# One chunk of a weight matrix, loaded behind a small write of VectorE

## The chip, the cores and the metric

The kernel runs on one core of one Trainium2 chip. The metric is the device time of one execution in microseconds, and its median over several runs. A core has five engines that each work through a queue of their own: TensorE (PE in the profile, with its weight loads as PEld), VectorE (DVE), ScalarE (ACT), GpSimd (POOL) and SyncE (SP). An engine waits for another by semaphores. Transfers between the device memory and the core's own memory are issued from the queues of SP, ACT and POOL, and carried by 16 DMA engines that all queues share.

## The reference

Inputs: x (8 x 1024 x 512), a condition (8 x 512), and weights. The first layer makes a matrix of its own for every one of the 8 batches, a base plus a term of rank 8; the second scales the columns and rows of a weight W by values made from the condition. Both are residual:

```
h = gelu(layernorm(cond) @ w1 + b1)
x_a, x_b = split(h @ w2 + b2)                    # 512 x 8 each, per batch
layer = base + x_a @ x_b.T                       # per batch
x = x + (x + x @ layer)
ys = cond / sqrt(512)
d = rsqrt((ys * ys) @ (W * W) + 1e-8)
x = x + ((x * ys) @ W) * d
```

Everything is float32. With I the identity, the whole of it is x @ P for each batch, with P = (2 I + base + x_a x_b^T) (I + diag(ys) W diag(d)).

## The kernel before

The kernel forms P for each batch and multiplies x by it. Float32 products are made of three: each operand is split into a rounded part (names with h, such as nh, bh, ph) and the rest (nl, bl, pl), and h x h, h x l and l x h are added up in the accumulators of PE. The rounded part is a copy or a scaled copy by ACT, the rest a subtraction by DVE. A matrix of 512 rows lies as 4 chunks of 128 rows, `[:, k, :]` for k = 0 to 3.

Up to line 886 the order of the instructions of ACT, DVE and SP is the order in the source: `ve`, `se` and `sy` are wrappers that pin each instruction behind the one before on the same engine (lines 52 to 64), and PE's matmuls are pinned by `mm` (line 44). Behind line 886, in the main part, the order on ACT, DVE and POOL is left to a planner. The framework sets all semaphores by itself, from what each instruction reads and writes; a transfer into a tile that an earlier instruction writes waits for that instruction, on the queue that issues the transfer.

The start, in the order of the source:

- Loads. From ACT's queue: chunk 0 of W into `w_sb` (line 89, 256 KB), and, behind ACT's first activation, chunk 1 (line 124, 256 KB). From SP's queue: `sm` (small things: the condition in columns, an identity), chunks 0 and 1 of the transposed base (`b_raw`), the condition, chunks 2 and 3 of W, chunks 2 and 3 of the base, and w1 (lines 90 to 97). Behind them on the same queue go the 16 loads of w2, 1 MB each, issued as buffers come free.
- Eleven matmuls on zeros (`keep_warm`, line 116), while the first loads are on their way.
- `ve.tensor_scalar_mul(ysT, condT, SCALE)` (line 180): ys, in columns.
- Chunk 0: POOL adds 2 I to the base's block (`twice_i`), ACT scales W's chunk by ys into `nh` (`round_yw`), ACT rounds the base into `bh` (`round_b`, for chunk 0 in three pieces), DVE makes `nl` (`rest_yw`) and `bl` (`rest_b`). Chunk 1 the same way (lines 188 to 192).
- Then ACT squares the four chunks of W into `wsq` (lines 193 and 194), and DVE makes ys squared and the layer norm of the condition; ACT's `sd` in it stands behind the squares.
- PE: twelve matmuls of chunk 0 into four accumulators `pg`, six of chunk 1 (two of the accumulators), then `pq_v` (`RowsProduct`, eight narrow matmuls that read `wsq`, for d), then the rest of chunk 1 with small transposes between, `pq_z` (for h), and chunks 2 and 3.

After that h is multiplied by w2 (the accumulators `px`, 128 narrow matmuls until about 61 us), P is formed for the first batches, and from about 72 us on the products of x with P (`po`) run, with the forming of the later P's between them. The stores of the output go out mostly from ACT's queue.

The change touches lines 124 (a load on ACT's queue, the second one of `w_sb`) and the place behind line 180.

Of the kernel before, what the change touches and what calls it, by code (L numbers as in the profile page):

```python
# [30 lines left out]
def cond_resid_kernel(ctx: ExitStack, tc: tile.TileContext, small, cond, condrows, consts,  # L31
# [32 lines left out]
    ve, se, sy = InOrder(nc.vector), InOrder(nc.scalar), InOrder(nc.sync)  # L64
# [18 lines left out]
    w_sb = cp.tile([P, KC, D], F32, name="w_sb")  # L83
# [37 lines left out]

    root = cp.tile([NB, 1], F32, name="root")
    se.activation(root, eps_l, AF.Sqrt)
    se.dma_start(w_sb[:, 1, :], weight[:, 1, :])


    hT = sp.tile([P, KC, 2, 32], F32, name="hT")
# [19 lines left out]
    def round_yw(k):  # L147

        se.mul(n0[k][0], w_sb[:, k, :], ysT[:, k, 0:1])
# [6 lines left out]
    def twice_i(k):  # L156
        blk = b_raw[:, k, k * P:(k + 1) * P]
        pin(nc.gpsimd.tensor_tensor(blk, blk, two_i, ALU.add))
# [19 lines left out]


    ve.tensor_scalar_mul(ysT, condT, SCALE)  # L180
    twice_i(0)
    round_yw(0)
    round_b(0, P, 2 * P)
# [1014 lines left out]
```

## Time and profile before

| | |
|---|---|
| time, median of 3 runs | 294.06 us (293.88 to 294.23) |
| time of the profiled execution | 293.74 us |
| its span, first to last instruction | 291.9 us |
| PE busy | 286.3 us (98%) |
| DVE, ACT, POOL busy | 214.8, 175.0, 35.9 us |
| mean granted clock of PE | 0.998 |
| DMA engines' share, 8 to 55 us | 1.00 to 1.04, at 404 to 438 GB/s |
| chunk 0 of W on ACT's queue: issued, time to landing | 0.73, 3.7 us |
| chunk 1 of W on ACT's queue: issued, time to landing | 1.24, 4.7 us |
| first main matmul (`po`) starts | 71.85 us |

A row of the timeline has the start in us, the length in us, the engine, the line, the operation, what it writes and reads, how many of its kind it stands for, and in brackets how long the engine was idle before it and what ended that. ACTq and SPq mark instructions that issue transfers. Almost everything in this kernel is issued through helpers, so the line is that of a helper (L62, L45), and tiles tell the groups apart; buffer numbers are left out. w_sb stands for W, and, where it comes from in_w, for w1. The profiled execution's own time is the span and 1.8 us around it.

### The profile page before, as it was taken

What the parts mean: (1) busy time and instruction counts of PE and PEld (TensorE: products, weight loads), DVE (VectorE), ACT (ScalarE), POOL (GpSimd) and SP (SyncE); (2) the same over time, 40 slices, a digit from 0 to 9 for tenths busy, and PEclk for the clock granted to TensorE, in tenths of its full rate; (3) what the DMA queues carried; (4) which work ended last, traced back from release to release, by engine and by line L of the source; (5) the groups of instructions that cost most, each with busy time, mean ns of one, the idle gap of its engine ahead of it and who ended that gap; (6) DMA issues with size and microseconds to landing.
All of it is one profiled execution on the core that took longest, in us unless ns stands there. A gap on an engine that the chain in (4) does not pass through costs nothing.

```text
span 291.9 us, 4100 instructions
## 1 busy us (share of the span) xinstructions
PE 286.3 (98%) x1519; PEld 225.2 (77%) x1519; DVE 214.8 (74%) x295; ACT 175.0 (60%) x272; POOL 35.9 (12%) x77
## 2 busy tenths in 40 slices
PE   7999999999999999999999999999999999999995
PEld 3665566467877878888877888887888889999994
DVE  2889898989916999519799565326789977798912
ACT  5757263286849884658654575544658745856641
POOL 2111000202944560000022000000000000000000
PEclk9999999999999999999999999999999999999999
DMA  7999999992799783332328114262175870852334
GB/s 209 405 429 413 411 403 405 390 383 90 187 321 322 235 250 116 110 145 93 159 80 263 55 72 135 83 216 74 72 251 176 291 257 1 290 204 87 142 146 144
DMA packets 19924, 62.14 MB, mean 213 GB/s; under 512 B 2736, under 2 KB 4016, under 8 KB 15552
## 3 DMA queue, kind: packets, MB, share of 16 engines
q1 hardware_dynamic: 9504, 43.76, 40.7%
q10 hardware_dynamic: 6912, 12.32, 11.5%
q0 software_dynamic: 3488, 5.79, 7.5%
q8 instruction: 12, 0.20, 0.3%
q14 instruction: 8, 0.07, 0.1%
HBM read 44.02 MB, written 17.84 MB: 212 GB/s over the span
## 4 chain that ended last, share of the span: by engine, by line
PE 96%; DMA 2%; ACT 0%; DVE 0%; SPq 0%; ACTq 0%; issue 0%
PE po L45 42%; PE pp L45 20%; PE sw L45 9%; PE px L45 5%; PE sz L45 5%; PE pg L45 4%; PE pq L45 4%; PE sv L45 2%; DMA b_raw<-in_baseT 2%; PE pr L45 1%; PE pt_t L45 1%; PE ps_t L45 0%; PE pq_v L45 0%; PE pq_z L45 0%; ACT o L62 0%; DVE o L62 0%
## 5 line engine op out<-in xcount | busy, mean ns | idle before, releaser
L45 PE MATMUL po<-ph,xs 128*128 128x512 f32 x352 | 113.7, 392 | 0.0
L45 PEld LDWEIGHTS po<-ph,xs 128*128 128x128 f32 x352 | 66.0, 188 | 15.6 <-issue 1.7
L45 PE MATMUL po<-pl,xs 128*128 128x512 f32 x176 | 68.6, 390 | 0.0
L62 ACT COPY o<-po 128x512 f32<-128x512 f32 x44 | 25.9, 588 | 35.0 <-PE po L45 35.0
L45 PEld LDWEIGHTS po<-pl,xs 128*128 128x128 f32 x176 | 33.0, 188 | 6.7
L62 DVE TENSOR_TENSOR xs<-x,xs 128x1024 fp32r<-128x1024 f32 (+1 forms) x23 | 27.0, 1176 | 15.0 <-ACT xs L62 15.0
L62 DVE TENSOR_TENSOR nl_p<-n,nh_p 128x1024 fp32r<-128x1024 f32 x21 | 25.7, 1222 | 12.4 <-ACT nh_p L62 12.4
L62 ACT CAST nh_p<-n 128x1024 fp32r<-128x1024 f32 x21 | 22.1, 1054 | 14.6 <-DVE n L62 10.9
L62 ACT CAST xs<-x 128x1024 fp32r<-128x1024 f32 x22 | 23.0, 1056 | 3.6 <-DMA x<-in_x 3.6
L62 ACT COPY q<-pp 128x512 f32<-128x512 f32 x30 | 17.4, 586 | 8.7 <-PE pp L45 8.6
L542 POOL DMA_DIRECT2D fa<-kept_a x28 | 13.8, 508 | 58.3 <-PE pr L45 54.0
L45 PE MATMUL pp<-nh_p,sh 128*128 128x512 f32 x48 | 19.0, 396 | 0.0
L45 PE MATMUL pp<-nh_p,sl 128*128 128x512 f32 x48 | 18.7, 390 | 0.0
L45 PE MATMUL pp<-nl_p,sh 128*128 128x512 f32 x48 | 18.7, 390 | 0.0
L62 DVE SCALAR_TENSOR_TENSOR n<-w_sb,ysT,d 128x512 f32<-128x512 f32 x24 | 16.9, 748 | 0.9 <-DMA d<-d_out 0.9
L62 ACT CAST sh<-sraw 128x1024 fp32r<-128x1024 f32 (+1 forms) x14 | 12.9, 926 | 6.8 <-DVE sraw L62 6.8
L62 DVE TENSOR_TENSOR sl<-sraw,sh 128x1024 fp32r<-128x1024 f32 (+1 forms) x14 | 14.9, 1067 | 2.2 <-ACT sh L62 2.2
L62 DVE TENSOR_TENSOR pl<-q,ph 128x1024 fp32r<-128x1024 f32 (+1 forms) x10 | 11.1, 1116 | 6.9 <-ACT ph L62 6.9
L45 PE MATMUL px<-w,hT 128*32 128x512 f32 x128 | 15.6, 599 | 0.0
L62 ACT COPY o<-sw 128x512 f32<-128x512 f32 (+1 forms) x12 | 6.2, 518 | 15.4 <-PE sw L45 12.3
L62 DVE TENSOR_TENSOR q<-pr,q 128x512 f32<-128x512 f32 x14 | 8.8, 688 | 7.9 <-PE pr L45 7.8
L62 DVE TENSOR_TENSOR n<-n,n 128x1024 f32<-128x1024 f32 x12 | 14.5, 1225 | 0.1
(199 smaller groups left out, 576.6 us busy)
## 6 DMA issues: line engine op xcount, KB each, us to landing
w<-in_w SPq DMA_DIRECT2D x16, 1024.0 KB, 10.4
x<-in_x SPq DMA_DIRECT2D x16, 1024.0 KB, 5.6
out<-o ACTq DMA_DIRECT2D x44, 256.0 KB, 2.3
out<-o SPq DMA_DIRECT2D x8, 512.0 KB, 2.9
fa<-kept_a POOLq DMA_DIRECT2D x28, 64.0 KB, 2.7
ft<-kept_t POOLq DMA_DIRECT2D x28, 64.0 KB, 3.5
d<-d_out POOLq DMA_DIRECT2D x6, 256.0 KB, 7.3
w_sb<-in_w SPq DMA_DIRECT2D x1, 1024.0 KB, 8.5
```

The source lines that it names most:

```text
L45: tc.keep_in_program_order(nc.tensor.matmul(*args, **kw))
L62: return lambda *a, **kw: pin(f(*a, **kw)) if InOrder.on else f(*a, **kw)
L542: nc.gpsimd.dma_start(fold[name, b][32 * c:32 * c + 32, :], kept[name, g][32 * i:32 * i + 32, :])
```

## The change

The load of W's chunk 1 leaves its place behind ACT's first activation. It now stands behind ys, with a memset by DVE of one element of the chunk (row 0, column 0) ahead of it. The load writes over that zero, so it has to wait for the memset, which on DVE stands behind the instruction that makes ys. On ACT's queue the load is now ahead of the first `round_yw`.

```diff
     root = cp.tile([NB, 1], F32, name="root")
     se.activation(root, eps_l, AF.Sqrt)
-    se.dma_start(w_sb[:, 1, :], weight[:, 1, :])
...
     ve.tensor_scalar_mul(ysT, condT, SCALE)
+
+    ve.memset(w_sb[:1, 1, :1], 0.0)
+    se.dma_start(w_sb[:, 1, :], weight[:, 1, :])
     twice_i(0)
     round_yw(0)
     round_b(0, P, 2 * P)
```

What is computed is the same, and so is the number of bytes that are moved.

## The prediction

> **What bounds the kernel now.** I read the chain that ended last first, then what TensorE (PE) waits for in the whole run, then the first 13 us of ScalarE (ACT), VectorE (DVE) and PE in order of time.
>
> ```profile
> PE 96%; DMA 2%; ACT 0%; DVE 0%; SPq 0%; ACTq 0%; issue 0%
> ```
>
> The chain, by engine: from the first real matmul on it is PE. Its start, by pieces (start, length):
>
> ```profile
> 1.16 4.56 DMA b_raw<-in_baseT
> 5.73 0.02 issue
> 5.75 0.31 ACT bh L62
> 6.06 0.04 issue
> 6.10 4.54 PE pg L45 x18
> 10.64 1.00 PE pq_v L45 x8
> 11.64 0.90 PE pg L45 x3
> ```
>
> PE's own waits, all of them (total, times, longest):
>
> ```profile
> PE pg L45 <- ACT bh L62: 1.1, 1, 1.1
> PE warm L45 <- DVE eps_l L62: 1.0, 1, 1.0
> ```
>
> After 6.10 us PE is never without work: whatever holds it back early moves everything behind it, up to the end at 291.9. So the question is how late PE becomes between 6 and 11 us, and ACT decides that:
>
> ```profile
> 1.24 0.39 ACTq L62 DMA_DIRECT2D w_sb<-in_weight  x1
> 2.48 0.20 ACT L62 ACTIVATE root<-eps_l 8x1 f32<-8x1 f32 x1
> 4.49 0.72 ACT L62 ACTIVATE nh<-w_sb,ysT 128x512 fp32r<-128x512 f32 x1 [1.81 <-DMA w_sb<-in_weight]
> 5.75 0.90 ACT L62 CAST bh<-b_raw 128x128 fp32r<-128x128 f32 x3 [0.54 <-DMA b_raw<-in_baseT]
> 6.56 0.72 ACT L62 ACTIVATE nh<-w_sb,ysT 128x512 fp32r<-128x512 f32 x1
> 7.73 0.62 ACT L62 CAST bh<-b_raw 128x512 fp32r<-128x512 f32 x1 [0.45 <-POOL b_raw L158]
> 8.26 2.19 ACT L62 ACTIVATE wsq<-w_sb 128x512 f32<-128x512 f32 x4
> ```
>
> The first row is the load that is moved. Its 256 KB landed 4.7 us after issue (the landing view for issues at 1.24), at 5.94, so the second nh at 6.56, which reads it, did not wait. The squares end at 10.45, pq_v starts at 10.57: it waits 0.4 us for them. Here the chain has no slack.
>
> **The change, part by part.** *Removed:* the issue at 1.24 (0.39 us of ACT's queue). ACT then loads a table until 2.46 and idles before 4.49, so that saves nothing.
>
> *Added on DVE:* one memset of one element. The rows of the small ones are 0.06 us; it runs behind ysT:
>
> ```profile
> 0.88 0.06 DVE L62 MEMSET eps_l<- 8x1 f32 x1
> 4.04 0.18 DVE L62 TENSOR_SCALAR ysT<-sm 128x32 f32<-128x32 f32 x1 [3.10 <-DMA sm<-in_small]
> ```
>
> So it is over at 4.22 + 0.06 = 4.28. DVE's next instruction (nl, at 5.24) waits for ACT's nh: 0.9 us of idle time cover it; without that cover it would cost 0.06.
>
> *Moved:* the load now waits on ACT's queue for the memset, and every instruction of ACT behind it waits too. That wait from 2.68 to 4.28 is mostly free, since the next one, nh, waits for chunk 0 until 4.43 anyway. Taking 0.04 us from engine to engine (ACT's bh ends 6.06, PE starts 6.10), the issue runs 4.32 to about 4.72, and nh starts at 4.75, not 4.49: 0.26 late. It ends at 5.47, while bh waits for b_raw until 5.75: hidden, with 0.28 to spare. If b_raw lands earlier, because the moved 256 KB no longer share its time on the DMA engines, PE can start at most 0.28 sooner; that gain is lost again at the next wait. SyncE's queue issues the same transfers: its first w1 load, at 4.42, waits for chunk 0 alone. Some later SyncE issue may reuse the completion counter of the moved load and wait for it, but by 8.5 us w1 and four w2 loads of 1 MB each have been issued there, and b_raw's second half ahead of them lands only at 10.5: the engines stay fed.
>
> *The landing.* What is late next is chunk 1. If it lands at T, the rows give: second nh at T + 0.06 (chunk 0: landed 4.43, nh 4.49); bh 0.62 later (12.79 to 13.41, the same pair without a wait); squares 0.53 after that (7.73 to 8.26), 2.19 long; pq_v 0.12 after their end. Sum: pq_v at T + 3.52, before 10.57, so PE is late by **T - 7.05**. The other way into PE, bh and then nl and bl on DVE (0.75 + 0.69), lets the last of the six pg matmuls ahead of pq_v start at T + 3.0: under 3.52, so the squares decide. What follows pq_v (sd, drow, pa, pt_v, pq_z) shifts with it: DVE's chain hangs on sd behind the squares, and PE has no hole to make good.
>
> *How long the load takes from 4.32.* The trace has no load on an ACT queue at this moment, so bounds:
>
> ```profile
> w_sb<-in_weight ACTq DMA_DIRECT2D x2, 256.0 KB, 4.2
> out<-o ACTq DMA_DIRECT2D x44, 256.0 KB, 2.3
> d<-d_out POOLq DMA_DIRECT2D x6, 256.0 KB, 7.3
> ```
>
> From below 2.3: 256 KB on ACT's queue while the engines are mostly free (T = 6.6). From above 7.0: the first d load, issued at 26.76 on a queue of its own beside SyncE's stream of w2, with all engines busy (T = 11.3, 4.3 late). And the engines are full when the moved load comes:
>
> ```profile
> 4.50:6.00 1.50, 0.53 (x3) 0.04 (x1) 0.75 (x1) 0.96 (x3) 0.14 (x1) 1.00 1.02 367
> 6.00:8.00 2.00, 1.90 (x8) 1.51 (x9) 1.31 (x2) 1.55 (x5) 0.93 (x2) 1.00 1.01 254
> ```
>
> (the last two columns: share of the 16 DMA engines, GB/s). So the near rows are the two loads of this very tile: 3.7 for chunk 0, on an empty queue beside SyncE's, and 4.7 for chunk 1, partly behind chunk 0. I take their median, 4.2, as an estimate between them: an empty queue speaks for 3.7, the larger backlog on SyncE's queue for 4.7. T = 4.32 + 4.2 = 8.5, PE late by 8.5 - 7.05 = **1.45 us** (3.7 gives 0.97, 4.7 gives 1.97).
>
> A rule speaks against this. The Trainium skill, "DMA: Bandwidth & Descriptors", section "Anatomy of one DMA", puts a transfer at about 2.0 us plus its bytes at 436 GB/s; for 256 KB that is an estimate of 2.6 us, T = 6.9 and no loss at all (-0.1 us). The rows of this stage, 3.7 and 4.7, do not agree, with the engines 100% busy; the rule is a fit for one transfer by itself, and on another queue.
>
> **The sum.** The profiled execution took 293.74 us (span 291.9 and 1.8 around it), 0.32 under the median of 294.06. 293.74 - 0 + 0 + 1.45 = 295.19; against the median, which the new runs will be compared with, 294.06 + 1.45 = **295.5**.
>
> **The rivals.**
> A (forecast): the load lands at 7.7 to 9.9, PE late by 0.65 to 2.85: 294.7 to 296.9. For: every transfer issued before 5 us whose landing is shown took 3.3 us or more, and the engines have no spare time until 60 us.
> B: it is hidden, and the kernel is not slower. The mechanism is the share of the DMA engines: with chunk 1 out of the way b_raw's two chunks land sooner (5.72 and 7.0 before), and chunk 1, alone on its queue, follows at once. It decides if the load takes under 2.7 us (T at or under 7.05). PE then starts up to 0.28 earlier and keeps it: 293.8 to 294.1; with 2.7 to 3.3 us it is a loss of 0 to 0.6 that can't be told from nothing. For: ACT's light-load row, 2.3. Against: the 254 GB/s at full engines in just these 2 us.
> C: the load comes behind the w2 stream as the d load does, 5.6 us and more: late by 2.9 to 4.3, 296.9 to 298.4. For: w1 with its 1 MB is issued at 4.42, 0.1 after it. Against: SyncE's queue still has b_raw and the second half of W ahead of w1 (landed 9.2 and 10.5 before), in shorter rows. In this case a page adds something: the skill's "TensorE: Matmul & The Clock Gate", section on HAM oscillation, says that some 3.4 us of idle PE halve its clock; at T = 11.3 PE would idle from about 9 to 12.6 (bh at T + 1.34), and by that page some 1.7 us might come on top. No row here shows it: the granted clock is 1.00 in each stretch I read.
> D: the change doesn't do what it says, that is, the memset runs in DVE's idle time from 0.94 on, and the load leaves at about 1.3 as before: 294.1. Against: both stand in hand-written order behind ysT, which waits for its own load until 4.04.
> E: the main part, where the order of ACT, DVE and POOL is not written by hand, is planned otherwise because the planner's start has moved, and gains over 0.6 us. For: nothing but the possibility; against: PE waits for nothing there. 293.4 or under.
>
> **How the numbers follow.** 0.2% of 294 is 0.59 us, about what a measurement of this kernel tells from no change. A 0.70, B 0.13, C 0.10, D 0.02, E 0.05. Faster by over 0.2% is E alone: 0.05. Within 0.2%: B's whole (load under 3.3 us) and D: 0.15. Slower: A and C, 0.80. The likeliest is A with 4.2 us: 295.5. For the range, A is 294.7 to 296.9; to leave out no more than 2 in 10 I go down to 294.3, into the upper end of B, and up to 297.1, C's beginning.
>
> **What would show it.** The issue of chunk 1 at 4.3 on ACT's queue, landing 8.0 to 9.0; ACT's second nh idle before it some 2 us, released by that DMA; PE with a hole of about 0.8 to 1 us ahead of its 13th pg matmul (before 9.07, then T + 1.34 = 9.8) and a second ahead of pq_v (12.0 against 10.57); from there the whole timeline parallel to the old one by the same 1.45 us, the px matmuls (19.70) and the first po matmul (71.85) too. If the landing is under 7.05, the step from row to duration was wrong. If PE is late at 12 us and not at 72, the claim that nothing behind has slack was wrong, and some wait for a w2 load (0.3 us in all now) or for x took it up. If w2 loads land later than before by more than the shift, the SyncE counter was no trifle.

## The result, and the profile after

| | before | after |
|---|---|---|
| median of 4 runs | 293.97 us (293.76 to 294.23) | 301.74 us (300.79 to 302.39) |
| ratio, 95% interval | | 1.0261 (1.0232 to 1.0290) |
| profiled execution | 293.74 us | 300.79 us |
| its span | 291.9 us | 299.0 us |
| mean granted clock | 0.998 | 0.988 |

The changed kernel is slower by 7.8 us, 2.6%. The forecast was slower by 1.45 us, at 295.5, with a range up to 297.1. The direction was right, the size five times too small, and the time lies outside the range. The profiled execution was the quickest of the four: it is 7.05 us slower than that of before, and it is the one explained here.

The chain that ended last, at its start (start, length):

```profile
4.16 7.91 DMA w_sb<-in_weight
...
12.11 0.60 issue
12.71 0.61 ACT bh L62
13.32 0.04 issue
13.37 2.96 PE pg L45 x6
16.32 1.87 PE pq_v L45 x8
18.19 1.32 PE pg L45 x3
```

Two things are new. The moved load takes 7.9 us from issue to landing, where it took 4.7 before and where I had put 4.2. And what PE does behind it takes longer: eight pq_v matmuls 1.87 us (1.00 before), three pg matmuls 1.32 us (0.90 before).

ACT in order of time, from the moved load on:

```profile
4.16 0.34 ACTq L62 DMA_DIRECT2D w_sb<-in_weight  x1
4.54 0.72 ACT L62 ACTIVATE nh<-w_sb,ysT 128x512 fp32r<-128x512 f32 x1 [1.87 <-DMA w_sb<-in_weight]
5.17 0.79 ACT L62 CAST bh<-b_raw 128x128 fp32r<-128x128 f32 x3
12.09 0.72 ACT L62 ACTIVATE nh<-w_sb,ysT 128x512 fp32r<-128x512 f32 x1 [6.12 <-DMA w_sb<-in_weight]
12.71 0.60 ACT L62 CAST bh<-b_raw 128x512 fp32r<-128x512 f32 x1
13.22 2.19 ACT L62 ACTIVATE wsq<-w_sb 128x512 f32<-128x512 f32 x4
```

The first nh starts 0.05 us later than before, and bh 0.58 us earlier, because the base's chunk 0 now lands sooner. Then ACT stands still for 6.12 us. PE's wait in the list of its waits is the image of that:

```profile
PE pg L45 <- ACT bh L62: 4.7, 1, 4.7
```

PE's clock in stretches of one us (from:to, length, then busy time and instructions of PE, PEld, DVE, ACT, POOL, then the granted clock, the DMA share and GB/s):

```profile
11.00:12.00 1.00, 0.00 (x0) 0.00 (x0) 0.00 (x0) 0.00 (x0) 0.00 (x0) 1.00 1.01 420
12.00:13.00 1.00, 0.00 (x0) 0.00 (x0) 0.16 (x1) 0.91 (x2) 0.00 (x0) 0.62 1.04 442
13.00:14.00 1.00, 0.63 (x2) 0.56 (x2) 1.00 (x2) 1.00 (x3) 0.00 (x0) 0.50 0.96 405
...
18.00:19.00 1.00, 1.00 (x6) 0.79 (x3) 0.00 (x0) 0.67 (x2) 0.00 (x0) 0.50 0.97 410
19.00:20.00 1.00, 1.00 (x7) 0.59 (x7) 0.12 (x1) 1.00 (x3) 0.00 (x0) 0.97 1.01 426
```

From 12.2 us on, 1.1 us before PE's hole ends, the clock is at half for 6.8 us (0.76 + 6 + 0.06, from the missing share of each stretch, doubled). From 20 us on the new timeline runs parallel to the old one: a pg matmul that started at 12.80 starts at 19.78, the first row of po matmuls in the chain at 79.06 instead of 72.01, and the last instruction ends 7.1 us later. So the loss is all made before 20 us, and nothing behind took any of it up.

### The profile page after: what moved, and what is told of

Same layout as the page of the kernel before. It is cut to its first block, busy times and chain, and to the rows that moved or that the text cites. A ratio compares the mean times of both kernels' runs of the same rounds, so it can differ in the third digit from the quotient of the medians.

```text
span 299.0 us, 4100 instructions
## 1 busy us (share of the span) xinstructions
PE 289.7 (97%) x1519; PEld 226.4 (76%) x1519; DVE 214.9 (72%) x296; ACT 174.9 (59%) x272; POOL 36.1 (12%) x77
## 4 chain that ended last, share of the span: by engine, by line
PE 94%; DMA 4%; ACT 0%; issue 0%; DVE 0%; ACTq 0%
PE po L45 41%; PE pp L45 20%; PE sw L45 9%; PE px L45 5%; PE sz L45 5%; PE pq L45 4%; PE pg L45 4%; DMA w_sb<-in_weight 3%; PE sv L45 2%; PE pr L45 1%; DMA sm<-in_small 1%; PE pq_v L45 1%; PE pt_t L45 1%; PE ps_t L45 0%; PE pq_z L45 0%
## 5 line engine op out<-in xcount | busy, mean ns | idle before, releaser
L62 ACT CAST nh_p<-n 128x1024 fp32r<-128x1024 f32 x21 | 22.1, 1052 | 13.0 <-DVE n L62 10.7
L62 ACT CAST sh<-sraw 128x1024 fp32r<-128x1024 f32 (+1 forms) x14 | 12.9, 925 | 6.8 <-DVE sraw L62 6.8
L62 ACT COPY o<-sw 128x512 f32<-128x512 f32 (+1 forms) x12 | 6.2, 520 | 15.4 <-PE sw L45 12.3
```

Source lines behind the costliest of these rows:

```text
L62: return lambda *a, **kw: pin(f(*a, **kw)) if InOrder.on else f(*a, **kw)
```

## Where the load was for 7.9 us

The trace keeps every packet of a transfer, with its queue. MB that ACT's queue moved in each us, in the kernels that follow too (chunk 0 is moved until 4 us; the rest is chunk 1):

| us | before | after | half late | nothing ahead | nothing behind |
|---|---|---|---|---|---|
| chunk 1 issued | 1.24 | 4.16 | 2.88 | 4.04 | 4.27 |
| 4 to 5 | 0.21 | 0 | 0 | 0 | 0 |
| 5 to 6 | 0.03 | 0 | 0 | 0.05 | 0 |
| 6 to 7 | 0 | 0 | 0 | 0.11 | 0 |
| 7 to 8 | 0 | 0 | 0.22 | 0.10 | 0 |
| 8 to 9 | 0 | 0.12 | 0.04 | 0 | 0.14 |
| 9 to 10 | 0 | 0.08 | 0 | 0 | 0.08 |
| 10 to 11 | 0 | 0.06 | 0 | 0 | 0.04 |
| landed | 5.9 | 12.1 | 10.2 | 8.7 | 11.0 |

In the changed kernel the first packet of chunk 1 starts at 7.81, 3.65 us after issue. Until then only SyncE's queue moves, 1.1 MB: what is left of the base's chunks 0 and 1, W's chunks 2 and 3 and part of the base's chunks 2 and 3, all issued before 4.16. From 7.81 to 11.22, where its last packet starts, the load moves beside w1 and the last rows of the base, and 0.84 us later it counts as landed. The middle part can be estimated: each of 16 engines has 8 rows of 2 KB for it at 0.084 us a packet, and if between two of them goes a row of w1, 8 KB at 0.309 us, that is 8 x 0.393 = 3.1 us. Rows can be put down to one engine where one starts within a few ns of another's end. Read so, a row of the load follows a row of the base 17 times, about once for each engine, and a row of the base follows one of the load once; load and w1 change places 145 times. This is the theory that the runs below test, **in turn**: a load waits until what was issued before it, on whichever queue, has moved, and then takes turns with what is moving beside it.

The trace of before had it already. Its landings come in the order of issue, over both queues:

| issued | 0.73 ACT | 1.16 SyncE | 1.24 ACT | 1.6 SyncE | 2.52 SyncE | 2.90 SyncE | 4.42 SyncE |
|---|---|---|---|---|---|---|---|
| load | W 0 | base 0 | W 1 | base 1 | W 2, 3 | base 2, 3 | w1 |
| landed | 4.43 | 5.72 | 5.94 | 7.0 | 9.22 | 10.5 | 12.9 |

A load issued at 4.3 fits into that row between 10.5 and 12.9.

## The experiments

Each was timed beside the kernel before on the same chip (medians 294.1 to 294.2).

**The write alone.** The memset goes up to the other small ones, the load stays where it was.

```diff
+    ve.memset(w_sb[:1, 1, :1], 0.0)
     root = cp.tile([NB, 1], F32, name="root")
     se.activation(root, eps_l, AF.Sqrt)
     se.dma_start(w_sb[:, 1, :], weight[:, 1, :])
```

> The same write of one zero and the same wait of the load for it, but the write stands ahead of ys, behind the other small memsets, so the load can leave at about 1.3 us as before. Both theories (the load is held up by what was issued before it; or it shares the DMA engines with what is issued after it) say: landing near 5.9, time 293.7 to 294.4, as before. If the write and the wait by themselves cost something, or the write into the tile changes the plan of the main part, the time stays near 301.7.

Measured: 294.01 us, ratio 0.9994 (0.9982 to 1.0006), load issued at 1.25, second nh at 6.45. The write and the wait for it cost nothing by themselves; what is left is the moment at which the load is issued.

**The hole filled.** The changed kernel with matmuls on zeros in PE's hole.

```diff
+    keep_warm(18)
     first_base(1, (0, 1))
```

> The changed kernel with 18 matmuls on zeros (about 4 us) put into PE's hole of 4.7 us ahead of chunk 1. Theory clock: the loss of 7.1 us is 5.0 for the late landing (12.07 - 7.05) and 2 for matmuls at half clock behind the hole. Then the landing stays near 12, the granted clock stays 1.00, pq_v starts at about 15.6 and the time is about 299 (5.0 over before). Rival: the 2 us come from the chain of ACT and DVE behind the landing, or the load lands later still in the unprofiled runs; then 301 to 302 with the clock at 1.00.

Measured: 299.95 us, ratio 1.0206 (1.0160 to 1.0251); single runs 299.15 (the profiled one), 299.93, 299.96 and 302.26, the last with a mean clock of 0.992, so there the clock seems to have fallen in spite of the filling. The load lands at 12.3, later by 0.25 than in the changed kernel. The first stretch and the last of those that were at half clock:

```profile
13.00:14.00 1.00, 0.38 (x2) 0.29 (x2) 0.91 (x2) 1.00 (x3) 0.00 (x0) 1.00 1.00 421
...
18.00:19.00 1.00, 1.00 (x6) 0.81 (x7) 0.97 (x4) 1.00 (x2) 0.00 (x0) 1.00 0.99 418
```

The clock stays at 1.00, pq_v starts at 15.62 (16.25 in the changed kernel) and the span is 297.4, 1.6 shorter although the load came later. So the half clock is a term of its own, of about 2 us (1.6, and the 0.25 of the later landing), and the lateness of the load the other.

**Nothing ahead.** The loads of chunks 2 and 3 of W and of the base wait behind ys as well.

```diff
+    ve.memset(w_sb[:1, 2, :1], 0.0)
+    sy.dma_start(w_sb[:, 2:4, :], weight[:, 2:4, :])
+    sy.dma_start(b_raw[:, 2:4, :], baseT[:, 2:4, :])
+    sy.dma_start(w1_sb, w1)
```

(behind the moved load; the same three lines at the top are taken out)

> The changed kernel, but the loads of W's chunks 2 and 3 and of the base's chunks 2 and 3 (1 MB together, on SyncE's queue) also wait behind ys, so that they are not issued before chunk 1. Theory in turn (the DMA engines serve the two queues in the order of issue, so the load lands behind the 1 MB issued before it): chunk 1, beside the chunk of W issued with it, lands 3.2 to 3.8 us after issue, at 7.4 to 8.0, and the time is 294.3 to 295.5. Theory late load (a load from ACT's queue at this moment takes about 8 us, because of what is issued behind it, w1 and w2 in long rows): landing near 12, time 300 or more.

Measured: 296.84 us from two runs, ratio 1.0087 (1.0055 to 1.0119).

```profile
4.04 0.36 ACTq L62 DMA_DIRECT2D w_sb<-in_weight  x1
4.45 0.72 ACT L62 ACTIVATE nh<-w_sb,ysT 128x512 fp32r<-128x512 f32 x1 [1.77 <-DVE w_sb L62]
5.07 0.79 ACT L62 CAST bh<-b_raw 128x128 fp32r<-128x128 f32 x3
8.74 0.72 ACT L62 ACTIVATE nh<-w_sb,ysT 128x512 fp32r<-128x512 f32 x1 [2.88 <-DMA w_sb<-in_weight]
```

Issued 0.12 us earlier and from the same queue, the load takes 4.7 us instead of 7.9 once the 1 MB ahead is gone: its first packet starts at 5.35. Read engine by engine as above, its rows now change places with the 4 KB rows issued just behind it, 242 times. The landing is still 0.7 us later than I expected, and the time 1.3 us over my bound; the clock was at half for 3.4 us in the profiled run, which I had not expected behind a hole of 1.5 us:

```profile
11.00:12.00 1.00, 1.00 (x4) 0.57 (x4) 0.93 (x4) 1.00 (x4) 0.78 (x2) 1.00 1.02 434
12.00:13.00 1.00, 1.00 (x9) 0.26 (x8) 0.61 (x5) 0.86 (x3) 0.00 (x0) 0.50 0.97 410
```

The hole lies from 8.5 to 10.0, so the clock falls when PE has been at work again for 2 us. The second run, 296.50 us, has a mean clock of 1.000. That the hole is the cause was not tested in this kernel.

**Half late.** The load waits for ACT's first activation, not for ys.

```diff
+    ve.tensor_scalar_mul(w_sb[:NB, 1, :1], root, 0.0)
     se.dma_start(w_sb[:, 1, :], weight[:, 1, :])
```

> The load waits for a zero that VectorE makes from ACT's first activation (over at 2.68), so it is issued at about 2.85, not 1.24 and not 4.16. Theory in turn: it lands behind W's chunks 2 and 3 (issued 2.51) and about with the base's chunks 2 and 3 (2.90), at 9.0 to 9.8, PE is late by 2.0 to 2.8 and the time is 296.0 to 296.8; PE's hole is 1.9 us or less and the clock stays 1.00. Theory share, as I predicted with it (4.2 us from issue, whatever is ahead): landing at 7.05, time 294.0.

Measured: 298.05 us, ratio 1.0123 (1.0092 to 1.0154).

```profile
2.88 0.37 ACTq L62 DMA_DIRECT2D w_sb<-in_weight  x1
...
10.27 0.72 ACT L62 ACTIVATE nh<-w_sb,ysT 128x512 fp32r<-128x512 f32 x1 [4.41 <-DMA w_sb<-in_weight]
```

1.64 us later at issue is 4.3 us later at landing. The load's first packet starts at 6.96, when most of W's chunks 2 and 3 has moved, and it lands just ahead of the base's chunks 2 and 3 (10.7), issued with it. In turn was right on the order, though the landing, at 10.25, is 0.45 us above its range; the share from issue on, with a landing at 7.05, was wrong. The time is 1.25 us over my range, in part by that landing and for the rest because the clock fell here too.

**Half late, filled.** The same with `keep_warm(11)` ahead of chunk 1's matmuls.

> The kernel with the load half late (issue 2.88, landing 10.25), with 11 matmuls on zeros, 2.5 us, in PE's hole of 2.7 us ahead of chunk 1. In the half late kernel the clock fell to half for 3.4 us behind that hole, though the hole is shorter than 3.4. Theory clock: filled, the clock stays at 1.00 and the profiled execution takes 1.5 to 2 us less, 296.6 to 297.2, that is the landing's lateness (3.2) over before. Rival: the half clock has another cause (the small holes between the six matmuls of chunk 1); then it falls again, and the time is 298 to 298.7.

Measured: 297.07 us, ratio 1.0109 (1.0091 to 1.0126), profiled run 296.97 against 298.66 without the filling. The half late kernel at its slowest, and then the filled one in the same stretch:

```profile
14.00:15.00 1.00, 1.00 (x6) 0.20 (x8) 0.80 (x6) 0.60 (x1) 0.00 (x0) 0.50 1.09 434
```

```profile
14.00:15.00 1.00, 1.00 (x10) 0.42 (x3) 0.86 (x5) 0.55 (x2) 0.00 (x0) 1.00 1.04 411
```

Filling a hole of 2.7 us is worth 1.7 us in the profiled runs, 0.2 of it by a landing that came sooner, and 1.0 us by the medians (the quickest run without filling, 296.79 us at a mean clock of 0.997, lost little to begin with): the clock theory holds for a short hole as well.

**Nothing behind.** The changed kernel, with w1 and so all of w2 held back until chunk 1's nl is made.

```diff
     rest_yw(1)
+    ve.memset(w1_sb[:1, 0, :1], 0.0)
+    sy.dma_start(w1_sb, w1)
     rest_b(1)
```

(taken out at the top)

> The changed kernel, but SyncE's load of w1, and so all that is queued behind it, waits until VectorE has made chunk 1's nl, so that nothing is issued behind chunk 1 while it moves. In the changed kernel ACT's queue moved its first bytes at about 7.9, 3.7 us after issue, and its last at about 11.3, beside the rows of w1. Theory in turn: the start stays at 7.9 (the 1 MB ahead is the same) and only the moving gets shorter, about 1 us, so the landing is 9.5 to 10.3. Theory share with what comes behind: the start comes at once (about 5.5), the landing at 7 to 8. The time itself is over 300, since w1 and w2 come 7 us late; it is not what is asked.

Measured: 299.42 us from two runs, ratio 1.0179 (1.0160 to 1.0198).

```profile
4.27 0.34 ACTq L62 DMA_DIRECT2D w_sb<-in_weight  x1
...
11.04 0.72 ACT L62 ACTIVATE nh<-w_sb,ysT 128x512 fp32r<-128x512 f32 x1 [4.97 <-DMA w_sb<-in_weight]
```

The start stays: first packet at 8.10. So what comes behind doesn't delay its start. But the load still moves for 2.5 us, not 1, and lands at 11.0, above my range: the last row of the base's chunks 2 and 3 starts only at 9.90 here, and the load's last packet at 10.62, that is one row of 0.159 and seven of 0.08 later. The landing goes by the slowest engine, not by the mean. The expectation on the time was wrong as well, and this is worth knowing: w1 leaves 8.3 us late,

```profile
12.60 0.33 SPq L62 DMA_DIRECT2D w_sb<-in_w  x1
```

and PE waits for it nowhere.

**The other queue.** The late load from SyncE's queue, ahead of w1.

```diff
     ve.memset(w_sb[:1, 1, :1], 0.0)
-    se.dma_start(w_sb[:, 1, :], weight[:, 1, :])
+    sy.dma_start(w_sb[:, 1, :], weight[:, 1, :])
+    sy.dma_start(w1_sb, w1)
```

(w1's line at the top is taken out)

> The changed kernel with the late load issued from SyncE's queue, behind the 1 MB of chunks 2 and 3 and ahead of w1. Theory in turn: it starts when the base's chunks 2 and 3 have moved, at about 8.3, moves without w1 beside it, and lands at 9.6 to 10.4; PE is late by 2.6 to 3.4 and, with some of the half clock, the time is 297 to 299.3. Rival: the wait is a property of ACT's queue; then from SyncE it lands before 8.5, or it takes its 7.9 us here too and lands at 12, with 301 or more.

Measured: 298.58 us from two runs, ratio 1.0151 (1.0132 to 1.0170); second nh at 10.68, so a landing at about 10.65, a little above my range. The wait is no property of ACT's queue. In SyncE's the load goes ahead of w1's rows instead of between them, which is 1.4 us earlier than in the changed kernel.

**Half ahead.** Only the base's chunks 2 and 3, and with them w1, go out behind ys too; W's chunks 2 and 3 stay at the top.

```diff
     se.dma_start(w_sb[:, 1, :], weight[:, 1, :])
+    ve.memset(b_raw[:1, 2, :1], 0.0)
+    sy.dma_start(b_raw[:, 2:4, :], baseT[:, 2:4, :])
+    sy.dma_start(w1_sb, w1)
```

(the last two are taken out at the top)

> The changed kernel, but only the base's chunks 2 and 3 (0.5 MB) wait behind ys too; W's chunks 2 and 3 (0.5 MB) are issued ahead of the late load as before. So chunk 1 is issued at about 4.1 with half as much ahead of it. Theory in turn, by the amount ahead: ACT's queue moves its first bytes when W's chunks 2 and 3 have nearly moved, at 6.6 to 7.2 (7.9 with 1 MB ahead, 5.4 with none), and beside the base's rows the load lands at 9.4 to 10.3; PE is late by 2.4 to 3.2, and with up to 2 us of half clock the time is 296.4 to 299.3. Rival, a fixed delay of about 3.75 us after issue whenever anything is ahead: first bytes at 7.9, landing near 11, time 299 or more.

Measured: 300.14 us, ratio 1.0188 (1.0151 to 1.0225).

```profile
4.47 0.37 ACTq L62 DMA_DIRECT2D w_sb<-in_weight  x1
...
12.94 0.72 ACT L62 ACTIVATE nh<-w_sb,ysT 128x512 fp32r<-128x512 f32 x1 [6.63 <-DMA w_sb<-in_weight]
```

The start is where in turn puts it, first packet at 6.87 (5.35 with nothing ahead, 7.81 with 1 MB). The landing is not: 12.9, later than with all of it ahead, and the time is over my range as well. From 7 to 11 us the engines' share is 0.81 to 0.99, but a row of 4 KB takes 0.23 to 0.32 us (the medians of each us) instead of 0.159, and one of 2 KB 0.13 to 0.29 instead of 0.084. From 6 to 11 us 1.1 MB moved; at 410 GB/s it would have been 2.05, so by an estimate from these rates the stretch cost 2.3 us, about what the landing misses. Such a slow stretch lies in every profile here, in that of before from 6 to 8 us (the 254 GB/s that the prediction quotes). It is longest in this run and with nothing ahead. What causes it stays open: the records show the packets, not what they wait for.

**Third in turn.** No write, no wait: chunk 1 on SyncE's queue behind the base's chunks 0 and 1.

```diff
     for k in range(2):
         sy.dma_start(b_raw[:, k, :], baseT[:, k, :])
+    sy.dma_start(w_sb[:, 1, :], weight[:, 1, :])
...
-    se.dma_start(w_sb[:, 1, :], weight[:, 1, :])
```

> No write and no wait: chunk 1 is loaded from SyncE's queue, third in turn behind the base's chunks 0 and 1 and ahead of everything larger. Theory in turn: the base's chunk 0 lands at about 5.0, not 5.72, so PE starts at 5.5 to 5.7; chunk 1 lands at 6.5 to 7.2, as late as PE can bear without loss (7.05), and the time is 293.3 to 294.1, the same as before or a little under it. Rival: a queue that shares with nothing is slower, chunk 1 lands at 8 or more, and the time is over 295.

Measured: 294.10 us from 11 runs, ratio 0.9999 (0.9989 to 1.0008).

```profile
6.70 0.72 ACT L62 ACTIVATE nh<-w_sb,ysT 128x512 fp32r<-128x512 f32 x1 [0.20 <-DMA w_sb<-in_weight]
```

Issued at 2.10, 0.86 us later than before, it lands at 6.67 and costs nothing, as in turn says: only one chunk of the base more was issued ahead of it, 0.9 MB in all where it was 0.6 before. PE starts at 5.47 and pq_v at 10.24 (10.57 before), but the span is shorter by 0.2 alone and the time can't be told from before. No run here beats the kernel before.

The profiled runs in one table, without the write alone, whose load leaves as before. N is the start of the second nh, and N - 7.11 the prediction's rule for how late PE becomes (late by T - 7.05, nh at T + 0.06); the rest is what the rule leaves of the longer span:

| kernel | N | N - 7.11 | span over 291.9 | rest | hole of PE | at half clock |
|---|---|---|---|---|---|---|
| after | 12.09 | 4.98 | 7.1 | 2.1 | 4.7 | 6.8 |
| half ahead | 12.94 | 5.83 | 7.4 | 1.6 | 5.2 | 6.8 |
| nothing behind | 11.04 | 3.93 | 5.4 | 1.5 | 3.3 | 3.4 |
| SyncE's queue | 10.68 | 3.57 | 4.6 | 1.0 | 3.6 | 3.4 |
| half late | 10.27 | 3.16 | 5.0 | 1.8 | 2.7 | 3.4 |
| nothing ahead | 8.74 | 1.63 | 3.5 | 1.9 | 1.5 | 3.4 |
| hole filled | 12.34 | 5.23 | 5.5 | 0.3 | 1.1 | 0 |
| half late, filled | 10.07 | 2.96 | 3.3 | 0.3 | none | 0 |
| third in turn | 6.70 | -0.41 | -0.2 | 0.2 | none | 0 |

Where the clock stays up, the rule holds to 0.3 us; where it falls, 1.0 to 2.1 us come on top.

## Why the prediction was wrong, point by point

- *What bounds the kernel:* right. PE has no slack behind 6 us, and the delay of 7 us goes through to the end.
- *The memset, the moved issue, the first nh:* right. The issue came at 4.16, not 4.32, since ys was ready 0.12 us sooner; the first nh was 0.05 late, hidden; bh and PE started 0.6 earlier, not 0.28 at most, and that was lost again.
- *How late PE becomes, T - 7.05:* right, within 0.3 us where the clock stays up.
- *How long the load takes from 4.32:* **here it failed.** I took 4.2 us, between the two loads of the same tile. Chunk 0 had little more than the small things beside it and chunk 1 had 0.6 MB issued ahead of it, and neither had rows of w1 between its own. "The larger backlog on SyncE's queue" was named and given 0.5 us at most; with 1.1 MB to be moved first, it is 3.65 us to the first packet (1.3 in the run with nothing ahead), 3.4 of moving beside w1 and 0.84 to the landing, 7.9 in all. That is 3.5 us of PE's lateness (T = 12.06 for 8.5).
- *The clock:* the other failure, 2.1 us. It stood in the prediction as a sentence on the Trainium skill beside rival C, for holes of some 3.4 us, and not in the sum. The hole was 4.7 us, so the rule would have fired, but the forecast had a hole of 0.8 to 1 us.
- *Rival C* had the mechanism in part, the load behind SyncE's stream, with a top of 298.4 by rows and 1.7 more by the page. What I held against it, that the base and W's second half were still ahead of w1, was the very thing that held the load up.
- *SyncE's completion counter:* some issues of w2 wait for the moved load (SyncE waited up to 4.8 us for it). It cost nothing: PE waits for no w2 load.
- *The rules of the Trainium skill.* The fit of "DMA: Bandwidth & Descriptors", section "Anatomy of one DMA" (an estimate of 2.6 us for 256 KB), was further off than my rows. The same page's section "Queues, rings and completion order" says that an engine takes turns between the queues it has work for, packet by packet. The second half of the load's way agrees (8 x 0.393 = 3.1 us against 3.4); in the first half no turns are seen, since for 3.65 us ACT's queue got no packet in, and whether the engines had the load by then the records don't show. "TensorE: Matmul & The Clock Gate", section "The HAM clock gate", has an idle window of about 3.4 us before the clock halves. Blocks of 3.4 us are what the runs show, one or two of them, but a hole of 2.7 us was enough in the half late kernel, and half clock came behind one of 1.5 us once.

## What to carry to other kernels

What these runs support is this. Price a load that is moved by its place in the order of issue, over all queues, and not by how long it took where it was: write down issue and landing of its neighbours, and see whether they land in turn. ACT's queue, empty but for this load, was no way past a megabyte issued earlier on SyncE's, and a load that left 3 us later landed 6 us later. Then look at the hole that this leaves in PE: here even 2.7 us of it brought 3.4 us at half clock, so the same cause is paid twice.

## What had not been expected of the hardware

- Half clock behind short holes: 1.5 us (nothing ahead, in one of two runs) and 2.7 us (half late; mean clock 0.992 to 0.994 in three of four runs, and 0.997 in the fourth, a value that runs of the kernel before show too). The clock falls 2.7 to 4.2 us after the hole begins, in the six profiled runs that show it, and in three of them PE is back at work by then. In the kernel before PE idles 1.07 us ahead of its first real matmul, and the clock stays at 1.00.
- w1 and all of w2, 17 MB, can start 8 us late without any wait of PE (nothing behind).
- A stretch of 2 to 5 us near the start in which the DMA engines are mostly busy and many of their packets take 1.5 to 2 times as long or more; its cause is open.
